# Pacing the adjacency loads, the slot tables and the weight fills of a two-layer graph-attention and expert kernel

## The chip, the cores and the metric

The kernel runs on one core of a Trainium2 chip. The metric is the device time of one execution in microseconds (us), as a median of several executions. The profile comes from one execution that was taken by the hardware profiler. The engines are TensorE (PE, with its weight loads shown apart as PEld), VectorE (DVE), ScalarE (ACT), GpSimd (POOL) and SyncE (SP). SP issues nearly all plain DMAs here; POOL issues the indirect ones.

## The reference, cut to what matters

There are 2708 tokens of 256 features, a 0/1 adjacency of 2708 x 2708, and two layers of the same build: a graph attention, then a mixture of eight experts of which each token takes two.

```python
# layer 0
x = x + elu(softmax(where(adj > 0, (q @ k.T) / 16, -9e15)) @ v)      # q, k, v of layernorm(x)
x = x + sum over a token's best 2 of 8 experts: weight * (gelu(LN(x) @ W1) @ W2)   # hidden 1024
# layer 1
H = layernorm(x) @ W_fc + b_fc
x = x + softmax(where(adj > 0, s_src[:, None] + s_dst[None, :], -1e9)) @ H
x = x + sum over a token's best 2 of 8 experts: prob * (gelu(LN(x) @ W1) @ W2)     # hidden 512
```

## The kernel before

Tokens lie in 22 tiles of up to 128 rows. The kernel runs through four stages in one program: attention of layer 0, experts of layer 0, attention of layer 1, experts of layer 1. In most of it the order of PE, ACT and DVE is the order in which the program is written, and SP's order always is; an instruction that waits holds what stands behind it on its engine.

**Attention of layer 0** (`layer0_attention`) walks over six blocks of queries (five of 512, the last of 148). In each block it walks over 22 key tiles, called key steps here: scores on PE (L578), exponent on ACT (L590), mask on DVE (L593), product with the values (L642), three key steps behind the scores. While one block runs, `masks_of` builds the transposed mask of the next block. It is a generator that is advanced once in a key step (`next(later_mask)`): it asks for two groups of adjacency rows (`load`, SP, L421 and L425; for the last block a DVE memset, L413, stands before each), and then in each of five steps compares one group (L438), transposes it (L444) and asks for the group two further on. At the same time a `Line` of finished tiles is advanced; each tile's routing (`route`) normalizes it, chooses two experts (up to `sel`, L1504), counts on PE with the running totals `seen` (L1509, L1510), and scatters the tile's rows into the experts' regions of a DRAM table `disp` (POOL, L1527).

**Attention of layer 1** (`layer1_attention`) walks over groups of 6, 6, 4, 3 and 3 query tiles, again with 22 key steps each. At the start of the third group `experts1.open` allocates the expert stage's tables and `grid_tables` fills them: POOL writes integer patterns (iota, L1169), DVE converts them (L1172) and derives three more small tables. In the same group a generator `fill` loads the weights of experts 0 to 3, one every four key steps. When 14 tiles are routed, `begin` is called, and its generator `begin_steps` is advanced once in a key step: `place_early` works out on DVE which expert and which rows of `disp` the first 20 slots take (`counts`, L1213 to L1231, then L1241 to L1273, then `weight_rows`), and then `fetch_rows` asks for the rows of the first three slots.

**Experts of layer 1** (`run`, `slots`). A slot is 128 rows of one expert. `fetch_rows(s)` reads the row number into an SP register and issues four DMAs of 32 KB (`xg`, L1722) and one of 1 KB (`who`, L1728); for slot 0 it adds a dependency on every scatter emitted so far (`behind_written`). The first 16 slots take experts 0 to 7 in turn, twice. `run` therefore loads experts 4 to 7 at its start, into space that the attention has just left (L1751, 1154 KB each). In a slot DVE transposes the rows of the next slot (L1773), PE multiplies with W1 (`up`, L1800), ACT applies the GELU (L1808), and PE multiplies the slot before with W2 (`down`, L1816); DVE scales the result (L1822) and POOL scatters it (L1828). Inside `down`, `fetch` keeps the rows six slots ahead and asks POOL for weights (L1703) from slot 16 on. The `Line` is advanced twice in a slot until all tiles are routed; then `place_grid` is advanced twice in a slot and places the remaining slots. Its first step counts on PE (L1213), and its `pads` are later written by SP (L1542).

```python
for s in range(AHEAD):          # begin_steps, own_norm False: AHEAD = 3
    rows_.append(fetch_rows(s))
...
def slot(s, s1):                # the order inside a slot
    hT, bias2 = up(w, xe, ...); xe = turned(s + 1); line.step()
    place_grid steps, once the line is empty
    down(*behind, fetch); line.step()
```

Of the kernel before, what the change touches and what calls it, by code (L numbers as in the profile page):

```python
# [9 lines left out]
F32 = mybir.dt.float32  # L10
# [96 lines left out]
def adj_ffn_kernel(ctx: ExitStack, tc: tile.TileContext, a: dict, out: bass.AP):  # L107
# [268 lines left out]
    def layer0_attention(line):  # L376
        with ExitStack() as scope, ExitStack() as until_last:
# [300 lines left out]
            for b, (b0, nb, ts_) in enumerate(BLOCKS):  # L678
# [14 lines left out]
                for k in range(NT):  # L693
# [39 lines left out]
                    if k == 0 or k >= 2:  # L733
                        next(later_mask, None)
# [386 lines left out]
    class Experts:  # L1121
# [41 lines left out]
        def grid_tables(self, n):  # L1163

            def table(name, shape, parts_):
                i = self.one.tile([P, shape], I32, name="table_i")
                t = self.one.tile([P, shape], F32, name=name)
                for s0, size, pattern, base in parts_:
                    nc.gpsimd.iota(  # L1169
                        i[:, s0 : s0 + size], pattern=pattern, base=base, channel_multiplier=0  # L1170
                    )
                nc.vector.tensor_copy(t, i)  # L1172
                return t

            slots = self.all_slots
            rounds = -(-slots // E)
            all_ = rounds * E
            end = self.often
            whole_ = (end - n) // E
            first = end - whole_ * E  # L1180
            assert n < first < end
            self.level = table("level", all_, [
                (0, all_, [[1, rounds], [0, E]], 0),
                (n, first - n, [[0, first - n]], whole_),
                (first, whole_ * E, [[-1, whole_], [0, E]], whole_ - 1),
                (end, all_ - end, [[0, all_ - end]], NT + 1),
            ])
            self.of_grid = table("of_grid", all_, [(0, all_, [[0, rounds], [1, E]], 0)])
            e0 = n // E * E
            self.early_row = self.one.tile([P, e0], F32, name="early_row")  # L1190
            nc.vector.tensor_scalar(
                self.early_row, self.level[:, :e0], float(P), -float(IDLE), op0=ALU.mult, op1=ALU.add
            )
            nc.vector.scalar_tensor_tensor(
                self.early_row, self.of_grid[:, :e0], float(CAP), self.early_row,
                op0=ALU.mult, op1=ALU.add,
            )
            nc.vector.tensor_copy(self.expert[:, :e0], self.of_grid[:, :e0])
            self.count = self.one.tile([P, slots - n], F32, name="count")
            nc.gpsimd.memset(self.count, 1.0)  # L1200
            self.depth = self.one.tile([P, E], F32, name="depth")
            depth = [len(range(n + (e - n) % E, end, E)) for e in range(E)]
            nc.gpsimd.memset(self.depth, float(min(depth)))
            more = [e for e in range(E) if depth[e] > min(depth)]
            assert more == list(range(more[0], more[-1] + 1))
            nc.gpsimd.memset(self.depth[:, more[0] : more[-1] + 1], float(max(depth)))
            self.counted = self.one.tile([P, E], BF16, name="counted")

        def counts(self, late):
# [4 lines left out]
            n_e = one.tile([P, E], F32, name=f"n_e{late}")  # L1214
            nc.vector.tensor_copy(n_e, ps[:, :E])
            if late:
                nc.tensor.matmul(ps[:, E : 2 * E], ones, self.counted, start=True, stop=True)
                self.n_done = one.tile([P, E], F32, name="n_done")
                nc.vector.tensor_copy(self.n_done, ps[:, E : 2 * E])
                end = one.tile([P, E], I32, name="end")  # L1220
                nc.vector.tensor_add(end, n_e, regions)
                self.pads = [partial(self.pad, end, e) for e in range(E)]
# [4 lines left out]
                whole[:, 1 - late : NT + 1 - late].unsqueeze(2).to_broadcast([P, NT, E]),  # L1227
                ALU.is_gt if late else ALU.is_ge,
            )
            self.chunks = one.tile([P, E], F32, name=f"chunks{late}")  # L1230
            nc.vector.tensor_reduce(self.chunks, tab.rearrange("p t e -> p e t"), AX.X, ALU.add)  # L1231

        def place_early(self, s0, s1):

            one = self.one
            yield from self.counts(False)
            yield
            rounds, more = divmod(s1, E)
            s1 -= more
            there = one.tile([P, rounds, E], F32, name="there")  # L1240
            nc.vector.tensor_tensor(  # L1241
                there, self.level[:, :s1].rearrange("p (a e) -> p a e", e=E),
                self.chunks.unsqueeze(1).to_broadcast([P, rounds, E]), ALU.is_lt,
            )
            there = there.rearrange("p a e -> p (a e)")
            nc.vector.tensor_mul(there, there, self.early_row)
            nc.vector.tensor_scalar(self.token_row[:, :s1], there, float(IDLE), None, ALU.add)
            yield

            one_more = one.tile([P, E], F32, name="one_more")  # L1250
            order = one.tile([P, E], F32, name="order")
            passed = one.tile([P, more, E], F32, name="passed_early")
            self.taken = one.tile([P, E], F32, name="taken")
            nc.vector.tensor_scalar(one_more, self.chunks, float(rounds), None, ALU.is_gt)
# [4 lines left out]
            )  # L1259
            expert = self.expert[:, s1 : s1 + more]  # L1260
# [4 lines left out]
            )  # L1265
            nc.vector.tensor_scalar(
                self.token_row[:, s1 : s1 + more], row, float(IDLE), None, ALU.min
            )
            yield
            nc.vector.scalar_tensor_tensor(  # L1270
                one_more, order, float(more), one_more, op0=ALU.is_le, op1=ALU.mult
            )
            nc.vector.scalar_tensor_tensor(  # L1273
                self.taken, self.chunks, float(rounds), one_more, op0=ALU.min, op1=ALU.add
            )
            self.weight_rows(s1, s1 + more)

        def place_grid(self, s0, s1):
# [3 lines left out]
            yield from self.counts(True)  # L1282
# [370 lines left out]
        def begin_steps(self):  # L1653
            yield
            self.begun = True
            place = self.place if self.own_norm else self.place_early
            yield from place(0, FULL_AFTER[self.early])
            self.rows_ = [self.fetch_rows(s) for s in range(AHEAD)]
            self.weights = []
            if self.own_norm:  # L1660
                yield
            if not self.own_norm:
                return
            for s in range(AHEAD):
                self.weights.append(self.fetch_weights(s))
                yield

        def open(self, likely=None, pace=None):
# [11 lines left out]
            if not self.own_norm:  # L1680
                self.grid_tables(FULL_AFTER[self.early])
            row = self.packed_weights[-1]
            self.ring = [self.one.tile([P, row], F32, name=f"ring{i}") for i in range(RING)]
            if not self.own_norm:
                return self.fill(likely, pace)
# [6 lines left out]
        def fill(self, likely, pace):  # L1692

            for i, e in enumerate(likely):
# [4 lines left out]
                yield  # L1699

# [35 lines left out]
        def run(self, line):  # L1736
            with (
# [5 lines left out]
                with ExitStack() as order:  # L1743
                    if not self.own_norm:
# [4 lines left out]
                        for e in range(RING, E):  # L1749
                            self.ring.append(more.tile([P, row], F32, name=f"ring{e}"))  # L1750
                            nc.sync.dma_start(  # L1751
                                self.ring[e], self.packed_weights[0][e * P : (e + 1) * P, :]
                            )
# [9 lines left out]
        def slots(self, two, ps_mm, ps_acc, line):  # L1763
# [85 lines left out]
            line.gap = 1 if own_norm else 2  # L1849
            placed, placing, behind, xe = False, None, None, None  # L1850

            def slot(s, s1):
# [28 lines left out]
                if not own_norm and not placed and (not line.busy() or s + AHEAD == n):  # L1881
# [3 lines left out]
                    for _ in range(2 if s + AHEAD < n else n):  # L1885
                        if next(placing, self) is self:
                            placed = True
                            break
                if behind is None:
# [186 lines left out]
```

## Time and profile before

| | us |
|---|---|
| median of three executions | 1196.48 (1192.17 to 1197.87) |
| the profiled execution, whole | 1184.94 |
| its span, first to last instruction | 1183.2 |
| PE busy in it | 1125.7 (95%) |
| DVE / ACT / POOL busy | 649.9 / 433.4 / 410.9 |
| mean granted PE clock | 0.988 of full |

The page gives the busy time of each engine, then the span in 40 slices of 29.6 us with a digit for each engine's busy share and for the granted clock of PE. A row of a timeline gives start, length, engine, line, operation, tiles, and in brackets the idle time of that engine before it with what ended it. A row of the stretches gives busy time and number of instructions of each engine, then the granted clock, the share of the DMA engines and GB/s. Layer 0's attention lies at 0 to 490 us, its experts to 815, layer 1's attention to 981, its experts to the end.

### The profile page before, as it was taken

What the parts mean: (1) busy time and instruction counts of PE and PEld (TensorE: products, weight loads), DVE (VectorE), ACT (ScalarE), POOL (GpSimd) and SP (SyncE); (2) the same over time, 40 slices, a digit from 0 to 9 for tenths busy, and PEclk for the clock granted to TensorE, in tenths of its full rate; (3) what the DMA queues carried; (4) which work ended last, traced back from release to release, by engine and by line L of the source; (5) the groups of instructions that cost most, each with busy time, mean ns of one, the idle gap of its engine ahead of it and who ended that gap; (6) DMA issues with size and microseconds to landing.
All of it is one profiled execution on the core that took longest, in us unless ns stands there. A gap on an engine that the chain in (4) does not pass through costs nothing. (4 is left out here: it accounts for less than half of the span.)

```text
span 1183.2 us, 20895 instructions
## 1 busy us (share of the span) xinstructions
PE 1125.7 (95%) x6417; PEld 913.3 (77%) x6417; DVE 649.9 (55%) x2403; ACT 433.4 (37%) x1260; POOL 410.9 (35%) x503
## 2 busy tenths in 40 slices
PE   8989999999999999999999999998999997999993
PEld 5665666666666575689999999996899886899993
DVE  5555777786877767653222222223876776722224
ACT  3222222222122222453333333332776665644441
POOL 3001212121212122343434343433654544555542
PEclk9999999999999999999999999999999998999997
DMA  9678677977846638479676936544001516477346
GB/s 215 138 164 207 173 176 175 232 175 196 218 93 184 160 100 314 148 209 259 181 195 161 335 77 184 139 140 101 12 1 38 209 50 229 116 245 231 84 112 247
DMA packets 199429, 195.88 MB, mean 166 GB/s; under 512 B 90939, under 2 KB 182548, under 8 KB 193288
## 3 DMA queue, kind: packets, MB, share of 16 engines
q1 hardware_dynamic: 174970, 123.97, 41.6%
q0 software_dynamic: 23872, 69.76, 18.5%
q8 instruction: 55, 0.90, 0.3%
q14 instruction: 70, 0.57, 0.2%
q10 hardware_dynamic: 462, 0.68, 0.2%
HBM read 246.19 MB, written 66.15 MB: 264 GB/s over the span
## 5 line engine op out<-in xcount | busy, mean ns | idle before, releaser
L1800 PEld LDWEIGHTS mm<-xe,ring 128*128 128x128 f32 x2192 | 260.3, 193 | 14.7 <-DVE xe L1773 6.9
L1800 PE MATMUL mm<-xe,ring 128*128 128x128 f32 x2192 | 262.7, 277 | 7.4 <-DVE xe L1773 6.1
L1816 PE MATMUL acc<-ring,hT 128*128 128x256 f32 x1096 | 253.8, 382 | 0.7 <-ACT hT L1808 0.7
L1808 ACT ACTIVATE hT<-mm,ring 128x128 f32<-128x128 f32 x548 | 156.2, 370 | 265.1 <-issue 144.6
L1816 PEld LDWEIGHTS acc<-ring,hT 128*128 128x128 f32 x1096 | 202.5, 191 | 25.4 <-ACT hT L1808 0.9
L642 PEld LDWEIGHTS acc<-v,p 128*128 128x128 f32 (+1 forms) x880 | 160.1, 190 | 62.7 <-issue 36.7
L642 PE MATMUL acc<-v,p 128*128 128x257 f32 (+1 forms) x880 | 202.7, 383 | 0.0
L578 PE MATMUL s<-g,xnT 128*128 128x512 f32 x420 | 201.7, 601 | 0.6 <-DVE mT L597 0.6
L1822 DVE SCALAR_TENSOR_TENSOR y<-acc,who,bias 128x256 f32<-128x256 f32 x92 | 44.5, 483 | 254.4 <-PE acc L1816 249.5
L1527 POOL DMA_INDIRECT disp<-row,to x88 | 90.9, 1033 | 260.0 <-DVE x L662 122.9
L280 POOL TENSOR_TENSOR ln_rs<-ln_rs,minus_half 128x2 f32<-128x2 f32 x88 | 67.3, 766 | 178.9 <-DVE ln_rs L276 127.0
L922 PE MATMUL acc<-parts,m 128*128 128x266 f32 x924 | 126.4, 293 | 0.1
L1703 POOL DMA_INDIRECT ring<-L_ffn_packed,weight_row x76 | 79.8, 1050 | 123.4 <-PE acc L1816 87.8
L922 PEld LDWEIGHTS acc<-parts,m 128*128 128x128 f32 x924 | 117.1, 185 | 4.2 <-ACT raw L949 0.9
L578 PEld LDWEIGHTS s<-g,xnT 128*128 128x128 f32 x420 | 77.3, 191 | 55.6 <-issue 50.3
L590 ACT ACTIVATE p<-s 128x512 f32<-128x512 f32 x105 | 62.1, 596 | 132.2 <-PE s L578 115.9
L1838 POOL DMA_INDIRECT xd<-y,who x45 | 71.6, 1592 | 111.7 <-DVE xe L1779 60.1
L593 DVE SCALAR_TENSOR_TENSOR p<-p,mT 128x512 f32<-128x512 f32 x100 | 70.9, 709 | 69.5 <-ACT p L590 69.4
L889 ACT CAST m<-mT 128x512 fp32r<-128x512 fp8e4 (+4 forms) x168 | 71.9, 476 | 9.8 <-PE acc L922 6.2
L1828 POOL DMA_INDIRECT xd<-y,who x47 | 50.1, 1065 | 32.8 <-DVE y L1822 17.4
L264 DVE SCALAR_TENSOR_TENSOR row<-x,wr_rows 128x256 f32<-128x256 f32 x128 | 54.3, 424 | 3.3
L1779 DVE TENSOR_SCALAR xe<-xe_raw,ring 128x128 f32<-128x128 f32 x90 | 27.4, 348 | 43.8 <-DMA ring<-L_ffn_packed,weight_row 42.8
(330 smaller groups left out, 1073.6 us busy)
## 6 DMA issues: line engine op xcount, KB each, us to landing
adj<-in_adj_dram SPq DMA_DIRECT2D x100, 256.0 KB
L_ffn_packed<-in_L_ffn_W_dram SPq DMA_DIRECT2D x32, 512.0 KB
xg<-disp SPq DMA_DIRECT2D x368, 32.0 KB
ring<-L_ffn_packed SPq DMA_DIRECT2D x8, 1154.0 KB
L_ffn_packed<-in_L_ffn_W_dram SPq DMA_DIRECT2D x32, 256.0 KB
neighbours<-mT SPq DMA_DIRECT2D x5, 1408.0 KB
mT<-neighbours SPq DMA_DIRECT2D x5, 1408.0 KB
ring<-L_ffn_packed SPq DMA_DIRECT2D x3, 2182.0 KB
```

The source lines that it names most:

```text
L280: nc.gpsimd.tensor_tensor(rs[:r, 1], rs[:r, 0], minus_half[:r], ALU.pow)
L578: nc.tensor.matmul(ps[:kr, :nb], xnT[:, c, k0 : k0 + kr], g[:, c, :nb], start=(c == 0), stop=(c == DC - 1 and k < KEYS),)
L593: nc.vector.scalar_tensor_tensor(p, p, LARGEST, mask, op0=ALU.min, op1=ALU.mult)
L642: nc.tensor.matmul(accs[j][:r], p[keys, q0 : q0 + r], v[keys, k, :], start=(k == 0), stop=(k == NT - 1),)
L889: nc.scalar.copy(m[:, : q1 - q0], MASKS[b].of_key(mTs[b], k)[:, q0 - b * BN : q1 - b * BN],)
L922: nc.tensor.matmul(acc[:r], masks[t], parts[:, k, i], start=(k == 0 and i == 0), stop=False,)
L1527: nc.gpsimd.indirect_dma_start(disp[:], bass.IndirectOffsetOnAxis(ap=to[:r, j : j + 1], axis=0), rows2[:r, j], None,)
L1703: nc.gpsimd.indirect_dma_start(w, None, packed[:], bass.IndirectOffsetOnAxis(ap=self.weight_row[:, s : s + 1], axis=0), bounds_check=E * P ...
L1800: nc.tensor.matmul(ps[:, i, :], w[:, c * hidden + f * P : c * hidden + (f + 1) * P], xe[:, c, :], start=(c == 0), stop=(c == DC - 1),)
L1808: nc.scalar.activation(hT[:, f, :], ps[:, i, :], AF.Gelu, bias=w[:, b1 + f : b1 + f + 1])
L1816: nc.tensor.matmul(ps, hT[:, f, :], w[:, w2 + f * D : w2 + (f + 1) * D], start=(f == 0), stop=(f == hc - 1),)
L1838: start = nc.gpsimd.indirect_dma_start(xd[:], at, y, None, bounds_check=N - 1, oob_is_err=False, compute_op=ALU.add)
```

## The change

It has five parts.

- In block 4 of layer 0's attention, the mask of the last block is advanced at key steps 2, 5, 8 and so on, instead of at 0, 2, 3, 4 and so on.
- `grid_tables` becomes a generator: at `open` it issues POOL's instructions, with an integer tile for each table; DVE's part (the conversions, then the three small tables as before) is issued by the second step of `fill`.
- `place_early` compares the counts with whole chunks directly instead of first counting chunks, and is spread over more steps: a yield stands after the counts, after the first row numbers, after the scan and compare, after the reduction, after `taken` is begun and after its sum. `place_grid` begins with two empty steps.
- `begin_steps` asks for the rows of six slots, one in a key step, instead of three in one.
- Experts 4 to 7 are loaded in halves, two halves in each of the first four slots, ahead of that slot's `fetch`, instead of all at the start of `run`.

```diff
-                    if k == 0 or k >= 2:
+                    if k % 3 == 2 if b == last - 1 else k == 0 or k >= 2:
                         next(later_mask, None)
...
         def grid_tables(self, n):
+            filled = []
             def table(name, shape, parts_):
-                i = self.one.tile([P, shape], I32, name="table_i")
+                i = self.one.tile([P, shape], I32, name=f"{name}_i")
...
-                nc.vector.tensor_copy(t, i)
+                filled.append((t, i))
                 return t
...
+            yield
+            for t, i in filled:
+                nc.vector.tensor_copy(t, i)
...
         def place_early(self, s0, s1):
-            yield from self.counts(False)
-            yield
             rounds, more = divmod(s1, E)
             s1 -= more
-            there = one.tile([P, rounds, E], F32, name="there")
+            ps = misc.tile([P, GROUP, P], F32, name="misc").rearrange("p g n -> p (g n)")
+            nc.tensor.matmul(ps[:, :E], ones, self.seen, start=True, stop=True)
+            n_e = one.tile([P, E], F32, name="n_early")
+            nc.vector.tensor_copy(n_e, ps[:, :E])
+            yield
+            there = one.tile([P, rounds + 1, E], F32, name="there")
             nc.vector.tensor_tensor(
-                there, self.level[:, :s1].rearrange("p (a e) -> p a e", e=E),
-                self.chunks.unsqueeze(1).to_broadcast([P, rounds, E]), ALU.is_lt,
-            )
...
+                there, n_e.unsqueeze(1).to_broadcast([P, rounds + 1, E]),
+                whole[:, 1 : rounds + 2].unsqueeze(2).to_broadcast([P, rounds + 1, E]), ALU.is_ge,
+            )
+            one_more = there[:, rounds]
...
+            for r in range(rounds):
+                nc.vector.tensor_add(self.taken, self.taken, there[:, r])
+            yield
             self.weight_rows(s1, s1 + more)
...
         def place_grid(self, s0, s1):
-            yield from self.counts(True)
+            yield
+            yield
+            yield from self.counts()
...
             yield from place(0, FULL_AFTER[self.early])
+            if not self.own_norm:
+                self.rows_ = []
+                for s in range(self.rows_ahead):
+                    self.rows_.append(self.fetch_rows(s))
+                    yield
+                return
...
                 nc.sync.dma_start(self.ring[i], self.packed_weights[0][e * P : (e + 1) * P, :])
                 yield
+                if tables:
+                    next(tables, None)
...
                         for e in range(RING, E):
                             self.ring.append(more.tile([P, row], F32, name=f"ring{e}"))
-                            nc.sync.dma_start(
-                                self.ring[e], self.packed_weights[0][e * P : (e + 1) * P, :]
-                            )
...
+            def fill(e, i):
+                w0, w1 = i * row // 2, (i + 1) * row // 2
+                nc.sync.dma_start(
+                    self.ring[e][:, w0:w1], self.packed_weights[0][e * P : (e + 1) * P, w0:w1]
+                )
+            fills = [] if own_norm else [(e, i) for e in range(RING, E) for i in range(2)]
...
+                for _ in range(2):
+                    if fills:
+                        fill(*fills.pop(0))
                 if behind is None:
                     fetch()
```

## The prediction

> **What bounds the kernel now.** I read the page's slices first, then stretches by engine around the seams, then the timeline at each hole of TensorE (PE), then the DMA queue's own waits.
>
> ```profile
> PE   8989999999999999999999999998999997999993
> PEclk9999999999999999999999999999999998999997
> ```
>
> PE is the bound nearly everywhere, so only stretches where it stands still, or runs at a lower clock, can give time back. The stretches (us; busy of PE, weight load, DVE, ACT, POOL; clock; DMA share; GB/s):
>
> ```profile
> 390.45:393.86 3.41, 1.08 (x5) 0.69 (x5) 1.33 (x7) 0.00 (x0) 0.00 (x0) 1.00 0.63 164
> 393.86:397.28 3.42, 2.93 (x6) 1.38 (x6) 2.88 (x12) 1.20 (x4) 0.00 (x0) 0.50 0.80 185
> 998.02:1004.85 6.83, 4.97 (x20) 4.70 (x21) 5.18 (x26) 1.61 (x2) 1.94 (x3) 0.50 0.30 62
> 1015.09:1018.50 3.41, 1.05 (x7) 0.76 (x5) 1.38 (x10) 3.35 (x7) 1.96 (x4) 1.00 0.63 145
> 1018.50:1021.91 3.41, 3.41 (x12) 2.89 (x12) 1.40 (x5) 1.48 (x5) 1.96 (x3) 0.50 0.36 67
> 1040.00:1056.00 16.00, 16.00 (x111) 15.02 (x110) 3.44 (x8) 7.21 (x25) 9.39 (x10) 1.00 0.99 345
> ```
>
> After each large hole comes a stretch at 0.50. The timeline names what ended each hole (start, length, what; in brackets the idle time before it and its releaser):
>
> ```profile
> 392.43 0.49 DVE L438 TENSOR_SCALAR m_rows<-adj 128x640 fp8e4<-128x640 int32 x1 [4.56 <-DMA adj<-in_adj_dram]
> 923.26 0.20 DVE L1172 CAST of_grid<-table_i 128x72 f32<-128x72 int32 x1 [2.79 <-POOL table_i L1169]
> 927.77 0.17 PE L1509 MATMUL misc<-sel,before 128*128 128x8 bf16 x1 [1.49 <-DVE sel L1504]
> 974.91 0.17 PE L1509 MATMUL misc<-sel,before 128*128 128x8 bf16 x1 [1.25 <-DVE sel L1504]
> 981.58 2.04 SPq L1751 DMA_DIRECT2D ring<-L_ffn_packed  x4
> 991.15 7.61 SPq L1722 DMA_DIRECT2D xg<-disp  x4
> 999.38 0.45 DVE L1773 STREAM_TRANSPOSE xe<-xg 128x256 f32<-128x256 f32 x1 [6.60 <-DMA xg<-disp]
> 1017.36 0.17 PE L1213 MATMUL misc<-seen,ones 128*128 128x8 bf16 x1 [2.10 <-DVE seen L1518]
> 1059.09 0.45 DVE L1773 STREAM_TRANSPOSE xe<-xg 128x256 f32<-128x256 f32 x1 [1.99 <-DMA xg<-disp]
> 1087.69 0.45 DVE L1773 STREAM_TRANSPOSE xe<-xg 128x256 f32<-128x256 f32 x1 [2.49 <-DMA xg<-disp]
> ```
>
> ```profile
> SPq L1722 <- DMA ring<-L_ffn_packed: 8.7, 3, 2.9
> ```
>
> See three holes: an adjacency load (392), the slot tables (923), the second layer's start (974 to 1018), where four 1154 KB fills sit ahead of slot 3's rows and the queue itself is then held 8.7 us. The last two DVE rows matter later: rows come just in time long after the seam.
>
> **A. Adjacency at every third key step.** PE's matmuls end at 391.54 (389.64 + 1.90); the next starts at 394.35: 2.81 us lost. Then 2.93 us of work at half clock: 1.46 more. A mask is made two of its steps after its load was asked for: two key steps of 3.45 us before, six (20.7 us) after, so the wait should go: **-4.3**. The masks cost the same; each is 0.49 + 0.34 + 0.17 us of DVE. Three of five now fall into 400 to 430, where DVE is busy 25.86 of 30 us; some of that is catching up after the wait. If that cover is gone, up to 3 us come back; a gain beyond the hole is excluded. SP waits at each load for DVE's memset; behind it are weight packing and x1's stores, which wait for DVE there already (SP idle 6.08 us before its store at 411.50). I take 0.
>
> Here the Trainium skill (TensorE: Matmul & The Clock Gate, "HAM oscillation") warns of gaps over about 3.4 us. By that the hole costs 2.81 alone, and so does the 2.10 us hole at 1015. The rows say otherwise: stretches of 3.41 us with PE busy 1.08 and 1.05 were enough. I price the clock from the rows.
>
> **B. Tables in small steps.** Before, the second iota waits for the first conversion, behind two scatters, and DVE waits 0.45 + 2.79 us; PE pays 1.49 plus 0.37 before a transpose. Now POOL writes two separate tiles; DVE's five instructions (0.20, 0.20, 0.17, 0.18, 0.17: 0.92 us) come at key step 4 of that group, where DVE's result goes into tail masks used only at the last key step. POOL has the same instructions without the wait. **-1.9**; bounds -1.9 and -1.0.
>
> **C. The seam, in order.**
> Early placement: from 968.93 to 972.69 DVE spends 3.3 us on it (without the row normalization between). After, some ten instructions of 0.2 us stand ahead of routing's step at key step 10, and five behind. `sel` comes about 1.4 us sooner: the 1.25 us hole goes.
> Rows: slot 0's are now asked for at key step 11, not 9. They wait for every scatter emitted so far, now also the pair of step 10 (974.38 and 975.72 before, 1.4 sooner after; a scatter's median to landing is 2.8): about 977.1 against 971.70. No row shows a fetch held this way; bounds are 972 (not held) and 984 (held by the next pair, 979.49 and 980.82, plus landing). I take 977.1, as the code adds the dependency explicitly.
> One slot's rows cost SP 3.03 us (971.70, 974.67, 977.82). Six end at 995.2, landing about 2 us after issue: 981, 984, 987, 990. Slots 0 to 3 start near 982, 984.5, 988.5 and 993, where slot 3 stood until 999.88. Row 1 lands at 984, and DVE, which transposes slots 0 and 1 first, stands until then; behind it are only that slot's routing steps, which POOL's scatters follow. The rows moved past the fills on SP gain what the fills lose; POOL's queue is unchanged in order.
> Weights: the fills of experts 4 to 7, asked for at 981.58 before, start behind these rows, at 995.3. Two halves issue in 0.9 us (four fills: 2.04); 1154 KB at the 390 GB/s of these fills is 3.0; about 1 to land: 1000.2. PE is out of work at about 996: a 4 us hole and half clock again (slot 3 took 6.05 us, the next 3.65). So slot 4 starts at 1000.2 instead of 1005.93. Further fills follow at 0.95 + 3.03 = 4.0 us, in time for slots of 3.65 to 4.5.
> Halving: the skill (DMA: Bandwidth & Descriptors, "Bandwidth") says to batch to 1 MiB or more. Halves of 577 KB at its fit (2.0 us + bytes/436 GB/s) take 3.4 us each; one after the other the pair would land 1.9 us later than mine, and so each of four slots could. But four transfers in flight moved at 390 GB/s in the trace, and the halves are issued 0.45 us apart. I charge issue only, and keep 0 to 1.9 us a slot for the range.
> Late placement begins one slot later (two more yields, two steps a slot), so the 2.10 us hole and its 1.7 us of half clock go. Slot 8: 1000.2 + 6.05 + 3 x 3.7 = 1017.4 against 1024.80: 7.4 sooner.
> What is late next: SP. Before, row 16 is issued at 1041.91. After: 977.1 + 16 x 3.03 + 3.8 (eight halves) + 4 x 2.1 (pads) = 1037.8, only 4.1 sooner (a pair of pads stretched the step from one slot's rows to the next from 3.03 to 5.15, 1018.20 to 1023.35; they now come one slot later). With DMA at 0.99, slot 17's rows were used 10 us after issue (1044.89, 1055.22); slot 18's transpose ended 0.4 us before PE needed it; slot 26's (1087.69) was late. So PE's lead shrinks to SP's 4.1, plus 0.3 that those slots already lost: **-4.4** for C.
>
> **Sum:** -4.3 - 1.9 - 4.4 = -10.6, against a profiled execution of 1184.94 (span 1183.2, 1.7 around it): 1174.3. The median of three runs is 1196.48, 11.5 above that execution; carrying the microseconds over: 1185.9, say **1186**.
>
> **Rivals.**
> 1. No give-back (0.22). Either rows keep pace and C yields 7.4 (total 13.6), or slot 0's rows are not held: fills start at 990, nothing waits for them, and ACT binds (1.28 + 1.14 + 1.28 + 0.4 + 0.5, about 4.5 us a slot while both table loads are needed): slot 8 at 1013, C 11.8, total 18. Middle 1180.5. Against: SP's row after 1018 is unbroken.
> 2. Half works (0.21). Either A's hole only moves to DVE, or weights 4 to 7 are each late with half clock each time, leaving C at 0: gain 2 to 6, about 1192.5. For it: fills start 14 us later than before. Against: DVE idled 6.1 us in 380 to 393.
> 3. Slower (0.07): SP itself is held behind the halves. Before, issuing behind fills took 7.61 us instead of 1.85. If SP spends 7.7 us a slot on slots 0 to 3 instead of 4.0, row 10 goes out at about 1026 instead of 1015.22; PE waits 11 us for rows, pays half clock twice (3 us), and A and B return 6.2: 1204. It decides from 6.5 us a slot ((4.1 + 6.2)/4 above 4.0). Against: at most one expert's bytes are now ahead of a slot's rows, before four.
>
> **Numbers.** The forecast has 0.50. A measurement of this kernel can tell about 0.5% (6 us) from no change. Faster: 0.47 + 0.22 + 0.07 = 0.76; within 0.5%: 0.03 + 0.135 + 0.015 = 0.18; slower: 0.06. The range 1178.5 to 1194 reaches from an 18 us gain to the weak end of rival 2.
>
> **What would show it.** A: no wait of L438 for adj, no 0.50 stretch near 394. B: no DVE idle at the table conversions, no 1.49 us hole. C: slot 0's first rows near 971 (both of A's and B's gains shift it from 977) and 3.0 us a slot; SP's waits for ring near 0; a hole of about 4 us before slot 4, ended by weights; none at the late counts; then DVE waits for xg near slots 16 to 18 and 24 to 26 longer than before. I am wrong if row 0 goes out at its token row's time, if slot 4 doesn't wait, or if rows never bind later.

## The result, and the profile after

| | before | after |
|---|---|---|
| median, us (15 runs each) | 1196.76 (1192.17 to 1204.47) | 1189.63 (1188.63 to 1194.66) |
| ratio | | 0.9938 [0.9919, 0.9957] |
| the profiled execution, us | 1184.94 | 1189.22 |
| its span, us | 1183.2 | 1187.4 |

The kernel is 7.1 us faster where 10.6 were forecast, and the time lies in the forecast's range. The two profiled executions say the opposite: the one of before was 11.8 us below its own median, the one of after is at its median. The two pages must therefore not be subtracted at the end of the span. They can be compared place by place, and a second profile of the unchanged kernel (below) shows what a common execution of it looks like. In what follows a hole is a stretch in which PE stands still, and half clock is a granted clock of 0.50.

The slices of the page after:

```profile
PE   8989999999999999999999999998999998879993
PEclk9999999999999999999999999999999999989997
```

The dip that stood at the second layer's start has become smaller and a deeper one stands two slices on, near 1040 to 1060. The stretches by engine (columns as before) around the places that the prediction named, and around two new ones:

```profile
388.00:394.00 6.00, 6.00 (x23) 3.70 (x22) 4.71 (x14) 1.41 (x3) 0.00 (x0) 1.00 0.76 193
465.86:469.27 3.41, 1.71 (x9) 0.79 (x8) 2.42 (x10) 1.12 (x4) 2.75 (x3) 1.00 0.58 124
469.27:476.10 6.83, 6.83 (x21) 3.86 (x20) 5.36 (x26) 1.10 (x6) 2.66 (x3) 0.50 0.34 104
1008.58:1011.99 3.41, 0.98 (x5) 0.53 (x3) 1.52 (x7) 2.10 (x5) 2.41 (x3) 1.00 0.98 330
1011.99:1015.41 3.42, 2.88 (x13) 2.91 (x14) 0.00 (x0) 0.51 (x1) 1.18 (x2) 0.50 0.54 143
1036.00:1052.00 16.00, 10.65 (x71) 9.33 (x69) 2.02 (x5) 4.32 (x14) 7.09 (x7) 1.00 0.99 352
1052.95:1059.78 6.83, 5.27 (x20) 4.92 (x21) 1.26 (x3) 1.90 (x6) 1.02 (x1) 0.50 0.28 56
```

From 388 to 394 PE is busy without a break: A's hole and its half clock are gone. From 1036 to 1052, where PE was full before, it is busy for 10.65 of 16 us, with the DMA engines full, and 6.83 us at half clock follow. The timeline after, at the same places (start, length, what; in brackets the idle time before it and its releaser):

```profile
391.26 0.49 DVE L438 TENSOR_SCALAR m_rows<-adj 128x640 fp8e4<-128x640 int32 x1
464.98 0.17 PE L1519 MATMUL misc<-sel,before 128*128 128x8 bf16 x1 [0.35 <-DVE p L1504]
925.67 0.19 DVE L1202 CAST level<-level_i 128x72 f32<-128x72 int32 x1
925.80 0.17 PE L1519 MATMUL misc<-sel,before 128*128 128x8 bf16 x1
969.61 1.92 SPq L1738 DMA_DIRECT2D xg<-disp  x4
970.93 1.03 POOL L1537 DMA_INDIRECT disp<-row,to  x1 [1.92 <-issue]
989.08 0.71 SPq L1865 DMA_DIRECT2D ring<-L_ffn_packed  x2
990.55 2.61 SPq L1738 DMA_DIRECT2D xg<-disp  x4
999.82 2.05 PE L1813 MATMUL mm<-xe,ring 128*128 128x128 f32 x16 [0.61 <-DMA ring<-L_ffn_packed]
1005.78 2.05 PE L1813 MATMUL mm<-xe,ring 128*128 128x128 f32 x16 [2.15 <-DMA ring<-L_ffn_packed]
1008.05 3.15 SPq L1738 DMA_DIRECT2D xg<-disp  x4
1012.53 1.83 PE L1813 MATMUL mm<-xe,ring 128*128 128x128 f32 x7 [2.97 <-DMA ring<-L_ffn_packed]
1054.01 0.45 DVE L1786 STREAM_TRANSPOSE xe<-xg 128x256 f32<-128x256 f32 x1 [9.86 <-DMA xg<-disp]
1054.51 1.86 PE L1813 MATMUL mm<-xe,ring 128*128 128x128 f32 x7 [6.89 <-DVE xe L1786]
```

Read in order: the mask no longer waits for its adjacency rows; the table conversions no longer wait, nor does PE beside them; slot 0's rows go out at 969.61; the weights of experts 5, 6 and 7 (slots 5, 6 and 7) are each late, by 0.6, 2.15 and 2.97 us, where one hole of 6.1 us stood. Slot 8 starts at 1018.12 instead of 1024.80. Then, at slot 16, DVE stands 9.86 us for its rows and PE 6.89 us for DVE. The waits in 960 to 1062 by what was waited for (total, times, longest), and below them what SP waited for at slot 0's rows (960 to 975):

```profile
DVE xe L1786 <- DMA xg<-disp: 13.8, 4, 9.9
PE mm L1813 <- DMA ring<-L_ffn_packed: 5.7, 3, 3.0
SPq L1738 <- DMA disp<-row,to: 0.7, 1, 0.7
```

Slot 17 starts at 1060.65; in the profile of before it was 1056.41. So a lead of 6.7 us at slot 8 has become a lag of 4.2 against that execution. Of the 6.7 us, 2.0 were there before the early placement began (the last transpose ahead of it is at 962.93 instead of 964.90).

### The profile page after: what moved, and what is told of

Read it like the earlier page. It is cut to its first block, busy times and chain, and to the rows that moved or that the text cites. A ratio compares the mean times of both kernels' runs of the same rounds, so it can differ in the third digit from the quotient of the medians.

```text
span 1187.4 us, 20904 instructions
## 1 busy us (share of the span) xinstructions
PE 1128.9 (95%) x6417; PEld 916.1 (77%) x6417; DVE 649.2 (55%) x2401; ACT 433.0 (36%) x1260; POOL 410.2 (35%) x503
## 5 line engine op out<-in xcount | busy, mean ns | idle before, releaser
L1719 POOL DMA_INDIRECT ring<-L_ffn_packed,weight_row x76 | 79.2, 1042 | 125.8 <-PE acc L1829 94.0
```

Of the source, the lines that this page charges most:

```text
L1719: nc.gpsimd.indirect_dma_start(w, None, packed[:], bass.IndirectOffsetOnAxis(ap=self.weight_row[:, s : s + 1], axis=0), bounds_check=E * P ...
```

## Experiments

All comparisons are of five rounds against the kernel before on the same chip: its median was 1193.84 us beside the first four kernels, 1200.44 beside the next four, 1196.87 beside the last four. Ratios are used for that reason.

### The parts alone, and the kernel before again

The unchanged kernel:

> The kernel before, unchanged, to see whether its one shown profile (1184.94 us) is typical of its medians (1196.76). Theory 1: that execution was a lucky one; a typical one has the same four holes (adjacency 2.8 us, tables 1.5, rows 6.1, late counts 2.1) and several more stretches at half clock, near 470 to 490 and late in the last stage, so about 1196 with a mean clock below 0.988. Theory 2: the profile is taken under other conditions than the timed runs and always reads some 10 us less, so it will show about 1185 again and the same holes and clocks. Ratio to itself 1.000 within 0.3%.

A alone (on the kernel before):

```diff
-                    if k == 0 or k >= 2:
+                    if k % 3 == 2 if b == last - 1 else k == 0 or k >= 2:
```

> Only the adjacency of the last block at every third key step; all else as before. Theory 1: the hole of 2.8 us near 391 and its half clock go (PE about 4.3 us earlier at 460), but half clock at the end of the attention can fall due instead; 2 to 4 us faster, ratio 0.997 to 0.998. Theory 2: the gain is lost wholly at the next seam, where a hole of 1.7 us is then judged by another 3.41 us window: ratio 1.000.

B alone: `grid_tables` as a generator with its own integer tiles, DVE's part issued by `fill`'s second step.

```diff
...
-                self.grid_tables(FULL_AFTER[self.early])
+                tables = self.grid_tables(FULL_AFTER[self.early])
+                next(tables)
...
```

> Only the slot tables split into POOL's part and a later DVE part; all else as before. Theory 1: the 1.5 us and 0.4 us holes near 926 go, 1.9 us faster up to the seam, and the seam and all behind it move as a whole: ratio 0.998. Theory 2: the seam's times hang on transfers, not on PE, and give the 1.9 us back: ratio 1.000.

C alone: the whole change with these two undone.

```diff
...
+                for s in range(self.rows_ahead):
+                    self.rows_.append(self.fetch_rows(s))
+                    yield
...
+                for _ in range(2):
+                    if fills:
+                        fill(*fills.pop(0))
...
```

> Early placement in small steps, rows of six slots ahead, fills in halves, late counts one slot later; adjacency and tables as before. Theory 1: slot 8 starts 5 us earlier than before, but slots 16 and 17 wait for rows that are held behind weight gathers (7 us and half clock, 10 us in all), so the profile shows a loss of about 5 us against an execution that has no such wait; yet before has such a wait too in its typical executions, so the median is 0 to 3 us faster: ratio 0.998 to 1.000. Theory 2: before never waits there; C alone is 4 to 6 us slower: ratio 1.004. Theory 3: C carries nearly all of the measured gain: ratio 0.994.

| kernel | median, us | ratio to before |
|---|---|---|
| before again | 1195.83 | 1.0009 [0.9986, 1.0033] |
| A alone | 1189.07 | 0.9957 [0.9938, 0.9975] |
| B alone | 1192.16 | 0.9980 [0.9955, 1.0005] |
| C alone | 1195.5 | 1.0004 [0.9980, 1.0028] |

A is worth 5.1 us (0.0043 x 1193.84), B 2.4, though B's interval holds zero. C shows no gain: its interval goes from 2.4 us faster to 3.3 slower, which excludes the 4.4 us that were forecast for it. The product of the three, 0.9941, agrees with the whole change's 0.9938. The profiled execution of the unchanged kernel took 1195.93 us, as much as its median, so profiling does not by itself make an execution fast. It shows, in its timeline, a wait that the profile of before did not have:

```profile
1003.96 3.79 PE L1800 MATMUL mm<-xe,ring 128*128 128x128 f32 x16 [6.03 <-DVE xe L1773]
1093.12 3.78 PE L1800 MATMUL mm<-xe,ring 128*128 128x128 f32 x16 [3.77 <-DVE xe L1773]
```

The first is the hole at the seam. The second is late rows at slot 25: 3.77 us. Times of 3.79 and 3.78 us for 16 matmuls, instead of 2.05, show the half clock behind both. In the profile that the prediction was read from, rows near there cost PE less than 0.2 us (slot 26 starts 3.67 us after slot 25, where the step is 3.51). The clock record has half clock at 84.54 to 91.36 and at 477.07 to 480.48 as well, where that of before has none. With the 6.83 us behind slot 25 that is 17.1 us at half clock, an estimate of 8.5 us lost, out of the 11.0 us between the two spans.

The other three executions without C have such a late row too, in order A alone, B alone, and A with B (below):

```profile
1090.36 2.05 PE L1800 MATMUL mm<-xe,ring 128*128 128x128 f32 x16 [2.07 <-DVE xe L1773]
1061.66 3.78 PE L1807 MATMUL mm<-xe,ring 128*128 128x128 f32 x16 [3.77 <-DVE xe L1780]
1056.37 3.78 PE L1807 MATMUL mm<-xe,ring 128*128 128x128 f32 x16 [3.37 <-DVE xe L1780]
```

So four of five executions without C lose 2 to 4 us to late rows at slot 16, 17 or 25, three of them with half clock behind; the one that the prediction was read from is the exception. C alone, in its timeline:

```profile
1055.89 3.79 PE L1806 MATMUL mm<-xe,ring 128*128 128x128 f32 x16 [6.45 <-DVE xe L1779]
1096.78 2.05 PE L1806 MATMUL mm<-xe,ring 128*128 128x128 f32 x16 [3.08 <-DVE xe L1779]
```

The 6.0 us hole at the seam is gone, 6.45 us at slot 15 have come, and slot 25 still waits 3.08 us.

### What makes the rows late: gathers or the queue of SP

Four edits of the changed kernel. In the first, the row numbers of every weight gather from slot 16 on are made to point out of bounds, so that no weights move:

```diff
+            back = ring if self.own_norm else 0
-                same[:, r0:s1], self.expert[:, r0:s1], self.expert[:, r0 - ring : s1 - ring],
+                same[:, r0:s1], self.expert[:, r0:s1], self.expert[:, r0 - back : s1 - back],
```

> The changed kernel, but from slot 16 of the second layer on no weights are fetched again: the row index of every such gather is set out of bounds, so a slot uses the weights that its buffer still holds (this part of the computation is left out). The gathers are still issued. Theory 1 (rows of slots 15 to 17 wait behind 1154 KB gathers): the DVE waits for xg near slot 16 and near slot 26 are gone, no hole of PE over 1 us after slot 8, 8 to 10 us faster than the changed kernel, ratio to before 0.985 to 0.988. Theory 2 (SP alone is late with asking, the traffic does not matter): slot 16 still waits 4 us or more, ratio 0.991 to 0.994.

In the second, ACT issues the half fills instead of SP; in the third, SP writes one pad a slot instead of two; the fourth has both:

```diff
-                nc.sync.dma_start(
+                nc.scalar.dma_start(
                     self.ring[e][:, w0:w1], self.packed_weights[0][e * P : (e + 1) * P, w0:w1]
...
-                    for _ in range(2 if s + AHEAD < n else E):
+                    for _ in range((2 if own_norm else 1) if s + AHEAD < n else E):
```

> The changed kernel with the eight half fills of experts 4 to 7 issued from ACT's queue instead of SP's, at the same places. Theory 1 (SP is the late engine: each pair of halves costs it 1 us of issuing and holds the rows behind in its queue): SP spends 3.2 us a slot on slots 0 to 3 instead of 4.7 to 6.4, weights 5 to 7 land in time (the holes of 0.6, 2.1 and 3.0 us go), row 16 is asked for some 7 us sooner, the hole at slot 16 shrinks from 6.9 to under 3 us; ratio 0.988 to 0.990. Theory 2 (bytes, not issuing, hold the rows): nothing moves but the issue times, ratio 0.993 to 0.995, and ACT loses up to 1 us.

> The changed kernel with one pad instead of two written by SP in each slot once the late placement has begun, so over eight slots instead of four; all still before slot 20's rows. Theory 1 (SP is late): a pad costs SP about 1.05 us, row 16 is asked for 4 us sooner, before the dense gathers, and slot 16 waits 2 to 4 us instead of 6.9; ratio 0.989 to 0.992. Theory 2 (bytes alone): slot 16 waits as long as before the edit, ratio 0.994.

> Both of these on the changed kernel: half fills from ACT's queue and one pad a slot. Theory 1: row 16 is asked for some 10 us sooner than in the changed kernel, no wait at slot 16 is left, PE's lead from the seam (6 us) is kept to the end: ratio 0.985 to 0.988. Theory 2 (bytes): 0.993 to 0.995; then the total DMA traffic of slots 13 to 18 sets the time.

| kernel | median, us | ratio to before |
|---|---|---|
| no weights gathered | 1176.55 | 0.9820 [0.9792, 0.9848] |
| fills from ACT | 1189.96 | 0.9929 [0.9902, 0.9957] |
| one pad a slot | 1192.1 | 0.9931 [0.9908, 0.9954] |
| both | 1192.19 | 0.9940 [0.9919, 0.9961] |

Without the gathers' bytes the same stretch of the timeline is full and the DMA engines are at 0.43:

```profile
1036.00:1052.00 16.00, 16.00 (x109) 14.97 (x108) 3.77 (x9) 7.67 (x25) 9.23 (x10) 1.00 0.43 96
```

From slot 8 on no hole over 1 us is left. The time falls by 1.2% of 1200.44 against the changed kernel: 14 us (0.9938 - 0.9820, and the two intervals lie apart), more than the 8 to 10 us expected. The rows of slot 16 went out at 1038.46, hardly sooner than in the changed kernel (1039.79), and were used 4.6 us later instead of 14.2, so what the gathers set is how long rows take to land. The three edits that relieve SP give nothing that can be told from the changed kernel's 0.9938. With one pad a slot row 16 is not asked for sooner (1040.47), and 5.36 us are still lost at slot 16. With the fills on ACT, their issue stands in ACT's own order, and PE waits for the GELU (timeline):

```profile
1002.85 3.37 PE L1829 MATMUL acc<-ring,hT 128*128 128x256 f32 x8 [4.60 <-ACT hT L1821]
```

ACT is idle for 5.07 us before that; a pair of halves is issued within this time, but the profile puts the wait down to a DMA, so whether the issue or late data held ACT is not shown. Slot 8 starts only at 1024.74 there, yet the time cannot be told from the changed kernel's.

With both edits row 16 is asked for 9 us sooner, at 1030.68, and slots 15 to 17 do not wait at all. The wait has moved: row 18, asked for at 1038.63, is used at 1054.39, and slots 18 and 26 wait 1.86 and 3.65 us, each with half clock behind it:

```profile
1030.68 1.62 SPq L1738 DMA_DIRECT2D xg<-disp  x4
1089.12 3.29 PE L1813 MATMUL mm<-xe,ring 128*128 128x128 f32 x16 [3.65 <-DVE xe L1786]
```

In this execution asking sooner saved the rows that were asked for before the gathers ran, and left later ones late. It is 5.1 us below its kernel's median, so common executions lose more.

### Where the lead goes, and a version that keeps more of it

Eight of the gathers move data. By POOL's issue times and the bytes of the packets (4.7 MB in 1036 to 1052 and again in 1072 to 1090, at 1154 KB each) they are those of slots 18 to 21 and 26 to 29, four in a row each time. Each is issued as soon as the slot eight before it has freed its buffer, so a faster PE starts them sooner. In the first of the next kernels each of the eight waits for a DVE copy of its row numbers, made two slots apart with one exception:

```diff
+                t = {} if own_norm else {12: 18, 14: 19, 16: 20, 17: 21, 20: 26, 22: 27, 24: 28, 26: 29}
+                t = t.get(s)
+                if t is not None and (t < n or placed):
+                    self.paced[t] = self.one.tile([P, 1], I32, name=f"paced{t}")
+                    nc.vector.tensor_copy(self.paced[t], self.weight_row[:, t : t + 1])
...
+            row_at = self.paced.get(s, self.weight_row[:, s : s + 1])
...
-                bass.IndirectOffsetOnAxis(ap=self.weight_row[:, s : s + 1], axis=0),
+                bass.IndirectOffsetOnAxis(ap=row_at, axis=0),
```

> Edit on the changed kernel: the eight weight gathers that move data (slots 18 to 21 and 26 to 29, 1154 KB each) each wait for a small DVE copy of their row numbers, made two slots apart (in slots 12, 14, 16, 17 and 20, 22, 24, 26), so that they no longer follow one another at once. Nothing is left out. Theory 1 (the seam's lead is given back because the rows' packets stand among four gathers in a row, DMA share 0.98 and over for 14 us twice): DMA share stays near 0.7 between 1034 and 1062, the 6.9 us hole before slot 16 shrinks to under 2 us and the waits near slot 26 go; time 1179 to 1184 against 1196.8 before, ratio 0.985 to 0.990, at most the 14 us that leaving the gathers out gave. Theory 2 (bytes and SP's backlog bind, however the gathers are spaced): rows of slots 16 to 18 are late as they were, or a delayed gather is itself late (PE waits for ring at slots 19 to 21); ratio 0.993 to 0.998.

The second is the kernel before with A and B, without C:

> The kernel before with the adjacency step and the slot tables' split, and nothing of the seam's change. Theory 1 (the seam's part nets zero, the parts add up): 0.9957 and 0.998 give 0.9937, the ratio of the whole change (0.9938); in the profile the holes near 998 (6.0 us) and 1018 (2.1 us) stay, and slots 16 to 18 wait less than in the changed kernel. Theory 2 (the seam's part is worth something once the others are in, as only then a lead reaches it): ratio 0.996 to 0.998.

The third loads whole weights, one in a slot; the fourth asks for three slots' rows ahead instead of six:

```diff
-            fills = [] if own_norm else [(e, i) for e in range(RING, E) for i in range(2)]
+            fills = [] if own_norm else [(e, i) for e in range(RING, E) for i in range(1)]
...
-                w0, w1 = i * row // 2, (i + 1) * row // 2
+                w0, w1 = 0, row
...
-                for _ in range(2):
+                for _ in range(1):
                     if fills:
...
-                for s in range(self.rows_ahead):
+                for s in range(AHEAD):
```

> Edit on the changed kernel: the weights of experts 4 to 7 are loaded whole (1154 KB), one in each of the first four slots, in place of two halves. Nothing is left out. Theory 1 (bytes bind, not the number of transfers): PE's hole before slot 6 (2.1 us) and slot 7 (3.0 us) stays within 1 us of what it was, SP's time a slot stays at 4.7 to 8 us, ratio 0.992 to 0.996. Theory 2 (two smaller transfers each land later, by up to 1.9 us a slot): the holes before slots 5 to 7 shrink by 1.9 us or more, ratio 0.990 to 0.992 unless the rows of slot 16 take it again. Theory 3 (halves let rows through): rows 6 to 9 go out later than 990.6, 996.3, 1002.7 and 1008.1 and land later; holes grow, ratio 0.996 to 0.999.

> Edit on the changed kernel: rows of three slots are asked for ahead of the expert stage, not six; all else as changed. Nothing is left out. Theory 1 (a lead made at the seam is swallowed at slots 16 and 26 whatever its size): a hole of 3 to 6 us returns near slots 3 to 5, as rows 3 to 5 stand among the halves, slot 8 starts 3 to 6 us later than 1018, and the hole before slot 16 shrinks by as much; ratio 0.992 to 0.996, the same as the changed kernel. Theory 2 (the seam's gain survives in part): 3 to 6 us slower than the changed kernel, ratio 0.997 to 0.999. Theory 3 (the fills, started 10 us sooner, are what was late): the holes before slots 6 and 7 go, no hole near slot 3 comes, ratio 0.988 to 0.991.

The columns from slot 8 on are read from the timelines of PE, SP and DVE (us): when slot 8 starts, PE's waits for rows at slots 15 to 17, the one slot of these three whose rows took longest from issue to DVE's use of them, and when slot 18 starts.

| kernel | median, us | ratio to before | slot 8 at | holes at slots 15 to 17 | row issued, used | slot 18 at |
|---|---|---|---|---|---|---|
| changed | 1189.63 | 0.9938 [0.9919, 0.9957] | 1018.12 | 0.97 + 6.89 | 1039.79, 1054.01 | 1064.16 |
| whole weights | 1187.09 | 0.9927 [0.9898, 0.9957] | 1014.93 | 9.55 | 1036.27, 1052.25 | 1061.26 |
| three rows ahead | 1186.16 | 0.9909 [0.9879, 0.9939] | 1012.02 | 10.80 | 1030.50, 1047.08 | 1060.68 |
| paced gathers | 1183.18 | 0.9884 [0.9849, 0.9919] | 1017.18 | 1.37 + 1.92 | 1034.38, 1042.81 | 1057.78 |
| A and B alone | 1188.9 | 0.9934 [0.9912, 0.9956] | 1021.22 | 3.37 | 1044.89, 1055.87 | 1062.87 |

Slot 8 comes 6.1 us sooner with three rows ahead than in the changed kernel, as the first fills go out at 979.73 instead of 989.08 and no weight is late; 3.5 us of that are left at slot 18, because the hole at slot 15 is 10.80 us:

```profile
979.73 0.82 SPq L1865 DMA_DIRECT2D ring<-L_ffn_packed  x2
1030.50 2.69 SPq L1738 DMA_DIRECT2D xg<-disp  x4
1047.08 0.45 DVE L1786 STREAM_TRANSPOSE xe<-xg 128x256 f32<-128x256 f32 x1 [13.29 <-DMA xg<-disp]
1047.58 2.72 PE L1813 MATMUL mm<-xe,ring 128*128 128x128 f32 x11 [10.80 <-DVE xe L1786]
```

I had expected a hole near slot 3 from this edit; none came, and the third of the theories was the one that met the seam and the ratio. Whole weights shorten the waits of slots 5 to 7 from 5.7 to 2.8 us. Slot 8 comes 3.2 us sooner, and 2.9 us of that are still there at slot 18, although slot 16's hole grows from 6.89 to 9.55 us. By the intervals neither kernel's time can be told from the changed kernel's.

A and B without C give the whole change's ratio, so C shows no gain with the others in either. Where its lead goes is seen best when every execution is counted from the same point before C, the last transpose ahead of the early placement. In the five executions without C (the two of before, A, B, A with B) slot 8 starts 59.7 to 60.3 us after it; with C it starts after 55.2 (the changed kernel) and 50.1 (C alone). Slot 30, behind all of the gathers that move data, starts after 137.5 to 144.2 without C, and after 143.4 and 139.9 with it. The lead of 5 to 10 us is gone there, within what executions differ by.

Pacing is the test of the cause, and it was met. Two stretches of the paced kernel, below them the second one of the changed kernel, and the rows of slot 16 in the paced kernel from issue to use:

```profile
1036.00:1052.00 16.00, 13.23 (x87) 11.71 (x85) 2.28 (x6) 5.87 (x19) 6.79 (x7) 1.00 0.72 223
1072.00:1090.00 18.00, 18.00 (x126) 16.97 (x126) 4.96 (x14) 7.81 (x25) 10.65 (x11) 1.00 0.75 230
1072.00:1090.00 18.00, 18.00 (x127) 16.97 (x126) 4.05 (x10) 7.68 (x25) 10.57 (x11) 1.00 0.97 324
1039.54 3.67 SPq L1739 DMA_DIRECT2D xg<-disp  x4
1044.66 0.45 DVE L1787 STREAM_TRANSPOSE xe<-xg 128x256 f32<-128x256 f32 x1 [0.98 <-DMA xg<-disp]
```

The DMA share is 0.72 and 0.75 against 0.99 and 0.97 in the changed kernel. Row 16 goes out only 0.25 us sooner, and is used 5.1 us later instead of 14.2. PE's holes at slots 15 to 17 fall from 7.9 to 3.3 us, and slot 18 starts 6.4 us sooner, of which 0.9 were there at slot 8. The bytes are the same; only their spacing differs. By the medians it is the fastest of the kernels that load all their weights, 6.4 us below the changed kernel, with the two intervals just touching at 0.9919; from three rows ahead it cannot be told. What stays are rows that DVE still waits for (timeline of the paced kernel):

```profile
1042.81 0.45 DVE L1787 STREAM_TRANSPOSE xe<-xg 128x256 f32<-128x256 f32 x1 [3.86 <-DMA xg<-disp]
1052.02 0.45 DVE L1787 STREAM_TRANSPOSE xe<-xg 128x256 f32<-128x256 f32 x1 [4.41 <-DMA xg<-disp]
```

The second is not held by pads: row 17 goes out at 1044.39, the last pad packet moves before 1043, and from 1047 to 1049 the packet records hold 84 packets of a gather and none of the rows. For the first, pads (129 KB each, on the rows' own queue) move in the same microseconds, and the two are not separated. A hole of 1.57 us also stays at slot 28. Pacing together with three rows ahead was not tried.

## Why the prediction was right, and where it was not

The time fell into the range because A and B held. C gave nothing that can be told, so the range was met without the largest of the three forecast gains, and in part because it is wide (1178.5 to 1194): 1189.63 is nearer to the middle of rival 2 (1192.5) than to the forecast (1186).

**A** was right in mechanism and size: -4.3 forecast, 5.1 measured (3.0 to 7.4 by the interval). The hole near 394 is in none of the profiles with A, and in B alone and C alone it is there (2.52 and 2.81 us). At the same matmul of the routing PE stands at 464.98 instead of 469.19, 4.2 us sooner. In this one execution the seam of layer 0 then took the gain back: behind the hole of 1.70 us there, which before has as well, 6.83 us at half clock followed. Half clock near there comes with A and without: before again, B alone and C alone have it too, for 3.4 to 6.8 us. Pricing the clock from the rows, against the Trainium skill (TensorE: Matmul & The Clock Gate, "HAM oscillation"), held: holes shorter than its 3.4 us were again enough (2.97 us in the stretch from 1008.58, half clock behind it).

**B** was right: -1.9 forecast, 2.4 measured alone. The ratio by itself cannot show it, but the trace does. The conversions wait for nothing, and from places where PE is level with before (822.04 and 822.05) to the last transpose before the early placement (962.93 against 964.90) it gains 2.0 us.

**C** is the term that was mis-sized: -4.4 forecast, no gain measured. Its steps:

- *Row 0 held by the scatters of key step 10 until 977.1*: wrong. It went out at 969.61, before that pair (970.93). It waited for its row number and then 0.7 us for a scatter that had been issued before (the last pair ahead of it is at 965.25 and 966.58). The hold exists, but not for the pair that was named.
- *Slot 4 waits 4 us for weights*: wrong in place. Slot 4 did not wait; slots 5, 6 and 7 did, 5.7 us together, with one window of 3.41 us at half clock.
- *Slot 8 7.4 us sooner, the hole at the late counts gone*: right in size, with luck. Counted from the transpose before the early placement it is 4.7 us in the changed kernel, and 6.4 to 9.8 in four others with the same seam (paced, no weights, one pad, C alone). But the fills started 6 us sooner than forecast and then went out more slowly, and the two errors offset each other.
- *SP 4.0 us a slot while halves are issued*: wrong. From row 6 to row 10 it took (1012.35 - 990.55)/4 = 5.45 us. Issuing one slot's rows took up to 3.15 us instead of 1.9 with weights ahead. From row 0 to row 16 the sum said 60.7 us; it was 70.2 (969.61 to 1039.79), and it had been 70.2 before (971.70 to 1041.91). The change took no time off SP between these rows; row 16 came 2.1 us sooner because row 0 did. Rival 3's mechanism was there, then, below its threshold of 6.5 us a slot.
- *Halves charged for their issue alone*: doubtful. With whole weights the waits of slots 5 to 7 are 2.8 us instead of 5.7, about a microsecond a slot, within the 0 to 1.9 that the prediction had left open. The fit behind the 1.9 is stated in the Trainium skill (DMA: Bandwidth & Descriptors, "Anatomy of one DMA — SWDGE (gpsimd) path") for DMAs that GpSimd issues, and these are issued by SP. The two times (0.9927 and 0.9938) cannot be told apart.
- *PE's lead shrinks by 3 us at slots 16 to 18, as rows come just in time*: the right place, and late rows as forecast, but the wrong size. The forecast let the lead shrink to what SP gains in issue time, with the 10 us from issue to use carried over. Row 16 was used 14.2 us after its issue; without the gathers' bytes it was 4.6 with nearly the same issue time. The wait brought two windows of half clock. Against the profile shown before, the loss from slot 8 to slot 17 is 10.9 us.

Behind the last step is the choice of base. I took rows that arrived just in time in one execution as the rule, and charged only the new lateness. Four of the five profiles without C lose time to late rows there, and at slot 30 the executions with C lie among those without it. That the gathers' traffic takes the lead is shown by leaving it out and by spacing it. That every lead is lost is not shown: three rows ahead and whole weights keep 3.5 and 2.9 us at slot 18. So the rival that gave C nothing (half works, 1192.5) named the right result for C with the wrong cause: late weights did not use up the lead.

The forecast gain, 10.6 us, misses C's 4.4, of which A and B together gave back 1.3.

## What to carry to other kernels

A lead gained ahead of a stretch that is bound by DMA can be lost in it: look for the next place where the DMA share is near full (0.97 to 0.99 here), and ask which small transfer must pass it. Prefetches that are issued as soon as a buffer is free came in bursts of four here; spacing them cost eight DVE copies of 0.11 us and gave 6.4 us by the medians, where the rework of the seam gave nothing that could be told. Before costing a change from one profile, compare that execution with the median: the one used here was 1% faster, and it lacked waits and half clock that the others had.

## What the runs showed of the hardware

- While gathers fill the DMA engines, small packets can move only about one for one with the gathers' large ones. In the changed kernel, 1043 to 1047, the packet records hold 37, 45, 42 and 44 packets of 9232 B of the gathers in the four microseconds, and on SP's queue 37, 45, 44 and 41 of 256 B (rows) and 1032 B (pads). One slot's rows are 512 packets of 256 B, 32 for each of 16 DMA engines; with one let through for each gather packet of 0.35 us that is an estimate of 11 us, and rows 16 and 17 took 14.2 and 10.4. In the microsecond from 1052, when the gathers' packets have ended, 472 packets of 256 B move. It can also be worse than one for one: 84 to 10 with three rows ahead (1040 to 1042), 84 to none in the paced kernel (1047 to 1049); why is not shown. The first agrees with the Trainium skill (DMA: Bandwidth & Descriptors, "Queues, rings and completion order"), where an engine goes round its queues packet by packet: a queue's share in bytes then follows its packet size.
- Half clock comes in whole windows of 3.41 us, except for the last stretch, which ends with the execution. The edges lie on one grid through an execution: in before, the stretches that begin at 393.86, 998.02 and 1018.50 are 177 and 6 windows apart. In the fourteen profiles, from 30 to 1160 us, each full-clock window in which PE was busy for 1.42 us or less was followed by half clock, and none in which it was busy for more than 2.03. Between the two the busy time does not decide: in the changed kernel 1.89 us (from 486.34) was followed by half clock and 1.49 us (from 1046.13) was not.
- Moving the eight half fills from SP's queue to ACT's gave no gain that can be told (0.9929 against 0.9938), and PE waited 4.60 and 2.33 us for ACT's results.
